# Cross attention's output projection of two batches at a time, in seven products of blocks instead of eight

## The chip, the cores and the metric

The kernel runs on one core of a Trainium2 chip. The core has five engines, each with its own in-order queue of instructions: TensorE (PE; its weight loads are listed as PEld), VectorE (DVE), ScalarE (ACT), GpSimd (POOL) and SyncE (SP), which here only issues DMA transfers. TensorE multiplies 128 x 128 blocks and writes into PSUM; the other engines read PSUM or SBUF. An instruction that needs another engine's result or a transfer waits on a semaphore at the head of its queue, and everything behind it on that queue waits too. The metric is the device time of one execution in microseconds (us), less is better. All numbers are float32.

## What is computed

Two decoder layers with the norm after each addition, for 8 batches of 128 tokens of 512 features. The part that matters here is the second layer's cross attention: 16 query heads of 96 features in 4 groups, keys and values from the context and the tokens (256 in all), an output projection, an addition and a layer norm, and after it a low-rank expert layer.

```
scores = einsum('bhqd,bksd->bhqs', q, k) / sqrt(96)
attn   = softmax(scores)
out    = einsum('bhqs,bksd->bhqd', attn, v)     # 16 heads x 96 = 1536 features
x      = layernorm(x + out @ Wo.T)              # Wo: 512 x 1536, the projection of this change
x      = layernorm(x + low_rank_experts(x))
```

## The kernel before

The program is written out in full by Python loops; the order on each engine comes from the order in the source and a scheduler that places instructions as their inputs are expected. `tc.issue_after(instruction)` ties the placing of what stands in it to an instruction. Tiles come from pools with a number of buffers per tag; a tile that reuses a buffer waits for the last reader.

The cross attention is the last stage, from about 537 us on. The loop `for b in range(B)` takes a batch in two steps `hh` of eight heads each. For each step:

- `Heads8` makes the scores on TensorE (`s_x`, line 931, 24 matmuls), `maxima` and `exps` make the softmax on DVE and ACT (lines 941 to 960), the last step of which is a transposition in blocks of 32 (line 960).
- `turn` (line 966) moves the result into the tile `pT` by 16 DMAs of 64 KB, issued by SP (in the last two batches by SP and ACT in turns). `pT` has one buffer.
- `Front` makes keys, values and queries for the next two batches in pieces (`pvx`, `pkx`, `pqx`, all through line 86), which are put between the other work by `nxt.go(n)`.

At the first step of batch b, `mix(b - 1)` finishes the batch before: `outputs` multiplies the whole `pT` by the values (`o_x`, line 976, 48 instructions) into the tile `oTx` (128 x 3 x 512, one buffer, copied out of PSUM by DVE, ACT and DVE at line 982), and `projected` multiplies `oTx` by the output weights in 12 matmuls of 512 columns (`pox`, line 993), adds the old x out of PSUM and normalizes (`add_norm`, lines 91 to 107). Each matmul is two instructions in the trace, as the data are float32. At the second step, `low_rank(b - 1)` does a piece of the low-rank layer for each of three batches: turning the tokens (`low_tokens`), scores (`low_scores`), turning the weighted heads (`low_turn`) and the last product, norm and store (`low_last`). The last two batches have an order of their own; the code after the loop finishes batches 6 and 7.

The output weights `w_X_o` are three tiles of 128 x 2048 (1 MB each), loaded by SP at line 67 when earlier weights have been used up, between 466 and 506 us, and they stay in SBUF to the end. GpSimd has no work in this stage except the small power of the norms (line 97).

Of the kernel before, what the change touches and what calls it, by code (L numbers as in the profile page):

```python
# [43 lines left out]
def decoder(ctx: ExitStack, tc: tile.TileContext, a: dict, out: bass.AP):  # L44
# [858 lines left out]
    layer.close()  # L903
    for k in ("q0", "q1", "q2"):
        wqs.append(weight4(f"X_{k}"))
    wos = [weight(f"X_o{i}").rearrange("p (c o) -> p c o", c=4) for i in range(3)]


    with stage("x1b", 2, side="right") as ap, stage("f1", 2, side="right") as fp:
# [9 lines left out]
        class Heads8:  # L919
# [42 lines left out]
            def turn(self, pT, queues=(nc.sync,)):  # L962
                e = self.e.rearrange("p (s j) h k -> p s j (h k)", s=2)
                for i in range(4):
                    for j in range(4):
                        queues[j % len(queues)].dma_start(
                            pT[32 * j : 32 * j + 32, :, i, self.h0 // 2, :], e[32 * i : 32 * i + 32, :, j, :]
                        )

# [17 lines left out]
        def projection(b, oT, between={}):  # L987

            po = bank(f"pox_{b}")
            for i in range(NX):  # L990
                n, h = divmod(i, G)
                w = wos[(h * NS + n) // 4][:, (h * NS + n) % 4, :]
                nc.tensor.matmul(po, lhsT=oT[:, n, h * P : (h + 1) * P], rhs=w, start=(i == 0), stop=(i == NX - 1))  # L993
                for piece in between.get(i, ()):
                    piece()
            return po

        def turned_low(b):
            xT = fp.tile([P, NC, P], F32, tag="xT", name=f"xTf1_{b}")
# [87 lines left out]
        def low_rank(b):  # L1087

            if b >= 2:
                low_turn(b - 2)  # L1090
            if b >= 1:
                low_scores(b - 1)
            low_tokens(b)
            if b >= 2:
                low_last(b - 2)

        def pT_tile(b):
            return ap.tile([P, 2, 4, 2, 8 * 32], F32, tag="pT", name=f"pT_x1_{b}", bufs=1)

        pTs, vs_x, oTs_x = {}, {}, {}  # L1100

        def outputs(b):
            oTs_x[b] = ap.tile([P, NS, 512], F32, tag="oT", name=f"oTx_{b}", bufs=1)
            mixed(b, vs_x.pop(b), pTs.pop(b), oTs_x[b])

        def projected(b, between={}):
            po = projection(b, oTs_x.pop(b), between)
            xs[b] = add_norm(xs[b], po, f"x1_{b}")

        def mix(b):  # L1110
            outputs(b)
            projected(b)

        for b in range(B):
            pr, j = divmod(b, 2)
            if j == 0 and b:
                front, nxt = nxt, upcoming
            toks = slice(j * P, (j + 1) * P)
            for hh in range(2):
                now = Heads8(front.qT[:, :, toks], front.kT[:, :, :, toks], 2 * hh, f"x1_{b}_{hh}")  # L1120
                now.maxima()
                now.exps(0)
                now.exps(1)
                if b < B - 2 and hh == 0:

                    nxt.go((4, 3)[j] if b < B - 3 else 2)
                    if b:
                        mix(b - 1)
                    pTs[b] = pT_tile(b)
                    now.turn(pTs[b])  # L1130
                elif b < B - 2:
                    if j == 1 and b < B - 3:

                        upcoming = Front(pr + 2)
                    now.turn(pTs[b])
                    nxt.go(2)
                    if b:
                        low_rank(b - 1)
# [187 lines left out]
def _layouts(i):  # L1326
# [47 lines left out]
    for j in range(3):  # L1374
        a[f"X_q{j}"] = _rows(wq[j])
        a[f"X_o{j}"] = _rows(wo[:, j])
    a["X_k"] = _rows(i["L1_xattn_Wk"].reshape(KV, NS, 32, D).transpose(1, 0, 2, 3).reshape(KV * XD, D))
    return {k: np.ascontiguousarray(v) for k, v in a.items()}

# [17 lines left out]
```

## Time and profile before

| what | value | how to read it |
|---|---|---|
| three runs | 876.8, 877.1, 878.6 us | median 877.12 |
| the profiled execution | 878.72 us | its span, first to last instruction, is 876.9 |
| granted TensorE clock | 0.995 | mean over the execution, 1 is full speed |
| `pqx` (line 86), 256 columns | 384 instructions, 84.9 us busy | busy time counts overlaps once |
| `pox` (line 993), 512 columns | 168 instructions, 74.1 us busy | seven batches of 24 instructions |
| `s_x` (line 931) | 768 instructions, 50.0 us busy | |
| `o_x` (line 976) | 384 instructions, 43.7 us busy | |
| `pT` on SP (line 966) | 224 issues of 64 KB | one issue keeps SP for 0.585 to 1.674 us, median 0.595 |

The profile is one execution. "Busy" of an engine is the time in which it has an instruction running; a line in the list of groups gives the program's line, engine, operation, output from inputs, shape, count, busy time, mean length of one and the idle time before them with what ended it. The chain of waits is followed back from the last instruction: at each step to what released it.

### The profile page before, as it was taken

How to read it: one execution, taken by the hardware profiler on the slowest of the kernel's cores; microseconds unless marked ns; L12 is line 12 of the kernel's file. 1: busy time of each engine (PE TensorE's matmuls, PEld its weight loads, DVE VectorE, ACT ScalarE, POOL GpSimd, SP SyncE). 2: the span in 40 equal slices, each digit the busy share in tenths (PEclk: the TensorE clock that was granted, in tenths of full speed). 3: DMA queues.
4: the chain of work that ended last, by engine and by line, in shares of the span. 5: the costliest groups of instructions: out<-in, count | busy, mean ns of one | idle time of the engine just before them, and what ended most of it. 6: DMA issues, size and time to landing. Idle time of an engine off the chain costs nothing.

```text
span 876.9 us, 17899 instructions
## 1 busy us (share of the span) xinstructions
PE 851.9 (97%) x6482; PEld 530.0 (60%) x6482; DVE 543.4 (62%) x2166; ACT 369.6 (42%) x1535; POOL 188.9 (22%) x267
## 2 busy tenths in 40 slices
PE   9999999999899999999999999999999999999996
PEld 5776655655445455555555687858475846576454
DVE  3656786776868657777778512734363545467654
ACT  3876574664223126766666403303121322224310
POOL 2500233123433214555555300000000000000000
PEclk9999999999999999999999999999999999999998
DMA  9700000130300002000004020331213121313340
GB/s 327 310 2 26 1 14 13 50 109 1 145 13 24 1 1 97 2 1 2 2 2 146 27 73 1 79 90 43 46 37 86 43 48 36 82 42 80 81 96 36
DMA packets 30073, 50.73 MB, mean 58 GB/s; under 512 B 5536, under 2 KB 22048, under 8 KB 28192
## 3 DMA queue, kind: packets, MB, share of 16 engines
q1 hardware_dynamic: 27424, 47.49, 18.1%
q10 hardware_dynamic: 2560, 2.10, 1.1%
q8 instruction: 51, 0.84, 0.4%
q14 instruction: 38, 0.31, 0.1%
HBM read 30.69 MB, written 2.10 MB: 37 GB/s over the span
## 4 chain that ended last, share of the span: by engine, by line
PE 64%; DVE 19%; ACT 11%; POOL 2%; issue 2%; DMA 1%; SPq 0%; ACTq 0%; POOLq 0%; DVEq 0%
PE pqx L86 10%; ACT e_a L197 7%; PE pox L993 7%; PE pkx L86 4%; PE pvx L86 4%; PE s_x L931 4%; PE o_x L976 4%; PE pq L86 3%; PE pk L86 3%; DVE e_a L184 3%; PE pv L86 3%; PE pof L618 2%; PE pt_a L228 2%; PE po L86 2%; PE s_a L165 2%
## 5 line engine op out<-in xcount | busy, mean ns | idle before, releaser
L197 ACT ACTIVATE e_a<-e_a,m_a 128x128 f32<-128x128 f32 (+1 forms) x512 | 184.7, 363 | 96.0 <-DVE m_a L184 96.0
L952 ACT ACTIVATE e_x<-s_x,m_x 128x256 f32<-128x256 f32 x128 | 58.7, 484 | 139.8 <-DVE m_x L942 123.4
L197 ACT ACTIVATION_READ_ACCUMULATOR e_a<-e_a,m_a 128x1 f32 x512 | 96.7, 189 | 0.0
L86 PE MATMUL pqx<-xTx,w_X_q 128*128 128x256 f32 x384 | 84.9, 380 | 0.0
L86 PEld LDWEIGHTS pqx<-xTx,w_X_q 128*128 128x128 f32 x384 | 72.6, 190 | 11.4 <-issue 1.8
L993 PE MATMUL pox<-w_X_o,oTx 128*128 128x512 f32 x168 | 74.1, 597 | 0.7 <-DVE oTx L982 0.6
L941 DVE TENSOR_REDUCE m_x<-s_x 128x4 f32<-128x1024 f32 x32 | 37.6, 1218 | 41.2 <-PE s_x L931 41.2
L97 POOL TENSOR_TENSOR rs_x<-ve_x,neghalf 128x1 f32<-128x1 f32 x7 | 3.9, 550 | 268.3 <-DVE ve_x L95 249.2
L211 POOL TENSOR_TENSOR e_a<-e_a,rc_a 128x512 f32<-128x512 f32 (+1 forms) x64 | 52.8, 847 | 33.8 <-DVE rc_a L208 18.8
L993 PEld LDWEIGHTS pox<-w_X_o,oTx 128*128 128x128 f32 x168 | 31.3, 190 | 40.9 <-issue 39.2
L228 PE MATMUL pt_a<-ident,e_a 128*128 128x128 f32 x384 | 48.4, 273 | 3.0 <-DVE m_a L184 3.0
L931 PE MATMUL s_x<-kTx,qTx 32*128 32x256 f32 x768 | 50.0, 385 | 0.8 <-ACT e_x L952 0.8
L228 PEld LDWEIGHTS pt_a<-ident,e_a 128*128 128x128 f32 x384 | 43.4, 140 | 11.9 <-issue 5.0
L184 DVE CUSTOM_DVE_ANT_0 e_a<-s_a,masks 128x128 f32<-128x128 f32 (+1 forms) x256 | 47.1, 253 | 4.4 <-PE s_a L165 3.1
L931 PEld LDWEIGHTS s_x<-kTx,qTx 32*128 32x128 f32 x768 | 39.0, 184 | 16.9 <-issue 11.7
L184 DVE CUSTOM_DVE_ANT_0 e_a<-s_a,alibi 128x128 f32<-128x128 f32 (+1 forms) x256 | 47.3, 253 | 1.4 <-PE s_a L165 1.3
L976 PE MATMUL o_x<-pT_x,vx 128*32 128x512 f32 x384 | 43.7, 595 | 1.8 <-issue 0.6
L184 DVE DVE_READ_ACCUMULATOR2_ANT m_a<- 128x1 f32 x512 | 42.6, 83 | 0.1
L960 DVE STREAM_TRANSPOSE e_x<-e_x 128x1024 f32<-128x1024 f32 x32 | 39.7, 1241 | 0.8
L165 PEld LDWEIGHTS s_a<-kbd,qT 32*64 32x64 f32 x1024 | 21.7, 131 | 29.0 <-issue 15.4
L959 DVE TENSOR_SCALAR e_x<-e_x,rc_x 128x256 f32<-128x256 f32 x128 | 36.3, 347 | 3.8 <-DVE rc_x L956 2.4
L838 ACT COPY qTx<-pqx 128x512 f32<-128x512 f32 x24 | 14.1, 595 | 55.1 <-PE pqx L86 54.8
(236 smaller groups left out, 1616.4 us busy)
## 6 DMA issues: line engine op xcount, KB each, us to landing
pT_x<-e_x SPq DMA_DIRECT2D x224, 64.0 KB, 2.0
w_X_q<-in_X_q SPq DMA_DIRECT2D x3, 1024.0 KB, 4.7
w_X_o<-in_X_o SPq DMA_DIRECT2D x3, 1024.0 KB, 4.9
w_L_Wv<-in_L_Wv SPq DMA_DIRECT2D x2, 1024.0 KB, 6.8
w_L_Wo<-in_L_Wo SPq DMA_DIRECT2D x2, 1024.0 KB, 8.6
x_in<-in_x SPq DMA_DIRECT2D x8, 256.0 KB, 9.0
ct<-in_ctx SPq DMA_DIRECT2D x8, 256.0 KB, 2.6
cT<-in_ctxT SPq DMA_DIRECT2D x4, 512.0 KB, 3.9
```

The costliest lines, as they stand in the source:

```text
L86: nc.tensor.matmul(ps, lhsT=l, rhs=r, start=(i == 0), stop=(i == n - 1))
L165: nc.tensor.matmul(s[r // 2][64 * u : 64 * u + 64, r % 2, cols], lhsT=qT[rows, 64 - 64 * part : P - 64 * part], rhs=kbd[rows, :, :keys], s ...
L184: self.scored = nc.vector.tensor_tensor_reduce(self.e[:, r, cols], s[i][:, r % 2, cols], bias(r, cols), -1.0, 3e38, ALU.add, ALU.min, self ...
L197: nc.scalar.activation(e[:, r, x, :], e[:, r, x, :], AF.Exp, scale=-1.0, bias=self.m[:, part, r, x : x + 1], accum_out=self.su[:, part, r, ...
L211: nc.gpsimd.tensor_tensor(e, e, bc(self.rc[:, part, rs, :].unsqueeze(3), list(e.shape)), ALU.mult)
L228: nc.tensor.transpose(pt[:, r, cols], self.e[:, 2 * i + r, cols], ident)
L931: nc.tensor.matmul(sc[g // 2][:, g % 2, u * 256 : (u + 1) * 256], lhsT=qT[rows, (h0 + u) * NS + n, :], rhs=kT[rows, n], start=(n == 0), st ...
L941: nc.vector.tensor_reduce(m, self.s[i], AX.X, ALU.max, negate=True)
L952: nc.scalar.activation(self.e[:, :, j, :], self.s[half][:, i, :].rearrange("p (a k) -> p a k", k=32), AF.Exp, bias=self.m[:, j : j + 1], s ...
L960: nc.vector.transpose(self.e[:, :, js, :], self.e[:, :, js, :])
L976: nc.tensor.matmul(po[32 * g : 32 * g + 32, :], lhsT=v[:, s, g * XD + 32 * n : g * XD + 32 * n + 32], rhs=pT[:, s].rearrange("p i h x -> p ...
L993: nc.tensor.matmul(po, lhsT=oT[:, n, h * P : (h + 1) * P], rhs=w, start=(i == 0), stop=(i == NX - 1))
```

## The change

Batches 0 with 1 and 2 with 3 are projected together. With the 1536 features split into two halves (the first two and the last two heads of each group), the 512 output columns into two halves, and the two batches as the rows, the product is one of 2 x 2 blocks, and it is done in seven block products with sums before and after (the Strassen-Winograd scheme) instead of eight. A block product is six matmuls of 256 columns. Batches 4 to 7 are projected as before.

The seven products need three blocks of the weights as they are (`X_ob`, laid out by the host) and four sums of blocks. The sums are formed on the chip in `form_sums`: three loads of the weights in another layout (`X_ot`) into the three slots, four subtractions on GpSimd for each slot, and three stores to a buffer in device memory. From there and from `X_ob` the products' right sides are streamed through the three slots of 8 matmuls each (`stream`). After the second pair, the plain weights `X_o` are loaded into the slots for batches 4 to 7 (`plain_outputs`).

`paired` does the seven products with the sums of the left side on GpSimd, copies of two products on ACT, and additions on DVE and GpSimd. `oTx` gets two buffers. In the loop, batch 0 ends its first step with `form_sums`, tied to the last of the first 16 DMAs into `pT`; the first step of batch 1 makes `outputs(0)` and starts the stream; the first steps of batches 2 and 4 make the outputs of the batch before and then the pair. The low-rank pieces move to the second steps of batches 2 to 5 (`LOWS`) and to batches 6 and 7.

```diff
-    wos = [weight(f"X_o{i}").rearrange("p (c o) -> p c o", c=4) for i in range(3)]
+    slots = [wp.tile([P, 2048], F32, tag="w", name=f"w_X_o_{i}") for i in range(3)]
+    wos = [t.rearrange("p (c o) -> p c o", c=4) for t in slots]
+    kept = ctx.enter_context(tc.tile_pool(name="kept", bufs=1, space=bass.MemoryType.DRAM))
+    weight_sums_kept = kept.tile([P, 4, 3, 512], F32, tag="ts", name="ts")
+    def form_sums():
+        for i, t in enumerate(slots):
+            nc.sync.dma_start(t, a["X_ot"][:, i])
+            b11, b12, b21, b22 = (t[:, j * 512 : (j + 1) * 512] for j in range(4))
+            nc.gpsimd.tensor_tensor(b11, b12, b11, ALU.subtract)
+            nc.gpsimd.tensor_tensor(b12, b22, b12, ALU.subtract)
+            nc.gpsimd.tensor_tensor(b22, b22, b11, ALU.subtract)
+            nc.gpsimd.tensor_tensor(b21, b21, b22, ALU.subtract)
+            nc.sync.dma_start(weight_sums_kept[:, :, i, :], t.rearrange("p (j o) -> p j o", j=4))
+
+    sums_flat = weight_sums_kept.rearrange("p j i o -> p (j i o)")
+    BLOCK = 6 * 256
+    T1, T3, T4, T2 = ((sums_flat, j * BLOCK) for j in range(4))
+    B11, B21, B22 = ((a["X_ob"], j * BLOCK) for j in range(3))
+    ORDER = [B11, T1, B21, T2, B22, T3, T4]
+
+    def stream(t):
+        lo, hi = 2048 * t, min(2048 * (t + 1), 7 * BLOCK)
+        while lo < hi:
+            block, off = divmod(lo, BLOCK)
+            n = min(hi - lo, BLOCK - off)
+            source, base = ORDER[block]
+            nc.sync.dma_start(slots[t % 3][:, lo - 2048 * t : lo - 2048 * t + n], source[:, base + off : base + off + n])
+            lo += n
+
+    def plain_outputs():
+        for i, t in enumerate(slots):
+            nc.sync.dma_start(t, a[f"X_o{i}"])
...
+        def paired(b0, b1):
+            o0, o1 = oTs_x.pop(b0), oTs_x.pop(b1)
+            x0, x1 = xs[b0], xs[b1]
...
+            def product(left):
+                ps = bank(f"pox_{b0}_{used[0]}")[:, :256]
+                for kk in range(6):
+                    h, n = divmod(kk, NS)
+                    t, u = divmod(used[0], 8)
+                    nc.tensor.matmul(
+                        ps, lhsT=left[:, n, h * P : (h + 1) * P], rhs=slots[t % 3][:, u * 256 : (u + 1) * 256],
+                        start=kk == 0, stop=kk == 5,
+                    )
+                    used[0] += 1
+                    if u == 7:
+                        if t < 3:
+                            stream(t + 3)
+                        elif t < 5 and not paired.last:
+                            stream(t - 3)
+                return ps
+
+            add(nc.gpsimd, s, o1[:, :, first], o1[:, :, second])
+            add(nc.gpsimd, o1[:, :, first], o0[:, :, first], o1[:, :, first], ALU.subtract)
+            nc.scalar.copy(p1, product(o0[:, :, first]))
+            nc.scalar.copy(p5, product(s))
+            add(nc.gpsimd, s, s, o0[:, :, first], ALU.subtract)
+            add(nc.gpsimd, x0[:, first], x0[:, first], p1)
+            add(nc.vector, r0[:, first], product(o0[:, :, second]), x0[:, first])
+            add(nc.gpsimd, o0[:, :, second], o0[:, :, second], s, ALU.subtract)
+            add(nc.vector, p1, product(s), p1)
+            add(nc.gpsimd, x0[:, second], x0[:, second], p5)
+            add(nc.gpsimd, x0[:, second], x0[:, second], p1)
+            add(nc.vector, r0[:, second], product(o0[:, :, second]), x0[:, second])
+            add(nc.gpsimd, x1[:, second], x1[:, second], p5)
+            add(nc.vector, p1, product(o1[:, :, first]), p1)
+            add(nc.gpsimd, x1[:, first], x1[:, first], p1)
+            add(nc.gpsimd, r1[:, second], x1[:, second], p1)
+            add(nc.vector, r1[:, first], product(o1[:, :, second]), x1[:, first])
+            if paired.last:
+                plain_outputs()
+            else:
+                stream(2)
+            for b, r in ((b0, r0), (b1, r1)):
+                mean, rs = moments(r, f"x1_{b}")
+                nc.vector.tensor_scalar(r, r, mean, rs, ALU.subtract, ALU.mult)
+                xs[b] = r
...
+        PAIRED = 4
+        LOWS = {
+            2: [lt(0), lt(1)],
+            3: [lsc(0), lsc(1)],
+            4: [lh(0), lh(1), lt(2), ll(0), lt(3), ll(1)],
+            5: [lsc(2), lsc(3), lt(4)],
+        }
...
-                    nxt.go((4, 3)[j] if b < B - 3 else 2)
-                    if b:
+                    if b > PAIRED:
+                        nxt.go((4, 3)[j] if b < B - 3 else 2)
                         mix(b - 1)
+                    elif b and not j:
+                        nxt.go(3)
+                        outputs(b - 1)
+                        nxt.go(1)
+                        paired.last = b == PAIRED
+                        paired(b - 2, b - 1)
+                    else:
+                        nxt.go((4, 3)[j])
+                        if b:
+                            outputs(b - 1)
+                        if b == 1:
+                            for t in range(3):
+                                stream(t)
                     pTs[b] = pT_tile(b)
                     now.turn(pTs[b])
+                    if not b:
+                        with tc.issue_after(now.moved.ins):
+                            form_sums()
...
-                    if b:
-                        low_rank(b - 1)
+                    for piece in LOWS.get(b, ()):
+                        piece()
...
-                    low_turn(b - 3)
-                    outputs(b - 1)
                     if b == B - 2:
+                        low_turn(B - 6)
+                        low_turn(B - 5)
+                        outputs(b - 1)
+                        low_last(B - 6)
                         low_scores(B - 4)
                         low_last(B - 5)
                     else:
+                        low_turn(B - 4)
+                        outputs(b - 1)
                         low_tokens(B - 3)
```

Here `lt`, `lsc`, `lh` and `ll` are `low_tokens`, `low_scores`, `low_turn` and `low_last`, and `add(engine, out, left, right, op)` is one `tensor_tensor` on that engine.

More of the change, by code (lines that the diff above doesn't have):

```diff
@@ L965, in turn @@
                     for j in range(4):
-                        queues[j % len(queues)].dma_start(
+                        self.moved = queues[j % len(queues)].dma_start(
                             pT[32 * j : 32 * j + 32, :, i, self.h0 // 2, :], e[32 * i : 32 * i + 32, :, j, :]
@@ L996, in projection @@
             return po
+        def paired(b0, b1):
+            o0, o1 = oTs_x.pop(b0), oTs_x.pop(b1)
+            x0, x1 = xs[b0], xs[b1]
+            first, second = slice(0, 256), slice(256, 512)
+            s = ap.tile([P, NS, 256], F32, tag="s", name=f"s_x1_{b0}", bufs=1)
+            p1, p5 = (ap.tile([P, 256], F32, tag=f"p{i}", name=f"p{i}_{b0}", bufs=1) for i in (1, 5))
+            r0, r1 = (xp.tile([P, D], F32, tag="x", name=f"x_x1_{b}") for b in (b0, b1))
+            add = lambda eng, o, l, r, op=ALU.add: eng.tensor_tensor(o, l, r, op)
+            used = [0]
+            def product(left):
[39 more added lines that the diff above has]
+                xs[b] = r
@@ L1085, in low_last @@
             last(b, low_sum(b, turned_lows.pop(b)))
[L1087 to L1095, printed above, removed]
         def pT_tile(b):
@@ L1102, in outputs @@
         def outputs(b):
-            oTs_x[b] = ap.tile([P, NS, 512], F32, tag="oT", name=f"oTx_{b}", bufs=1)
+            oTs_x[b] = ap.tile([P, NS, 512], F32, tag="oT", name=f"oTx_{b}", bufs=2)
             mixed(b, vs_x.pop(b), pTs.pop(b), oTs_x[b])
@@ L1112, in mix @@
             projected(b)
+        PAIRED = 4
+        lt, lsc, lh, ll = ((lambda b, f=f: lambda: f(b)) for f in (low_tokens, low_scores, low_turn, low_last))
+        LOWS = {
[4 more added lines that the diff above has]
+        }
         for b in range(B):
@@ L1376, in _layouts @@
         a[f"X_o{j}"] = _rows(wo[:, j])
+    o = np.concatenate([a[f"X_o{j}"].reshape(P, 4, 2, 256) for j in range(3)], axis=1).reshape(P, 2, 6, 2, 256)
+    o = o.transpose(0, 1, 3, 2, 4)
+    a["X_ob"] = np.concatenate([o[:, 0, 0], o[:, 1, 0], o[:, 1, 1]], axis=1).reshape(P, -1)
+    a["X_ot"] = o.reshape(P, 4, 3, 512).transpose(0, 2, 1, 3).reshape(P, 3, 2048)
     a["X_k"] = _rows(i["L1_xattn_Wk"].reshape(KV, NS, 32, D).transpose(1, 0, 2, 3).reshape(KV * XD, D))
```

## The prediction

> **What bounds the kernel now.** I read the page's busy table first, then the chain of waits from 560 us on, then the timelines of SP and DVE, then the groups by shape on POOL, because the change adds work on SP and POOL while it takes work off PE.
>
> ```profile
> PE 851.9 (97%) x6482; PEld 530.0 (60%) x6482; DVE 543.4 (62%) x2166; ACT 369.6 (42%) x1535; POOL 188.9 (22%) x267
> ```
> ```profile
> 567.41 6.91 PE pqx L86 x32
> 574.32 5.31 PE o_x L976 x48
> 579.63 10.50 PE pox L993 x24
> 590.12 2.80 PE s_x L931 x48
> ```
> The first line is busy time by engine; the others are the chain that ended last (start, length, what). PE is never idle for more than a fraction of a microsecond here, so a product taken out shortens the kernel by its own length, and a wait put in front of PE lengthens it by its own length. The projection of one batch (pox) is 10.5 us.
>
> ```profile
> 550.15 22.55 SPq L966 DMA_DIRECT2D pT_x<-e_x  x32
> 572.80 0.53 SPq L795 DMA_DIRECT2D cT<-in_ctxT  x1
> ```
> ```profile
> 560.17 1.25 DVE L960 STREAM_TRANSPOSE e_x<-e_x 128x1024 f32<-128x1024 f32 x1
> ```
> ```profile
> pT_x<-e_x SPq DMA_DIRECT2D x224, 64.0 KB, 2.0
> w_X_o<-in_X_o SPq DMA_DIRECT2D x3, 1024.0 KB, 4.9
> ```
> These are SP's timeline, DVE's timeline and the DMA issues with their time from issue to landing. SP hands out the 32 pieces of pT for batch 0 at 22.55/32 = 0.705 us each: 16 for the first half of the heads, 16 for the second. The second half's input is ready at 561.4 (DVE's transpose), just when the first 16 are through (550.15 + 11.3). The last issue starts at about 572.1 and lands 2.0 later, at 574.1; o_x, which reads all of pT, starts at 574.3. So SP is as close to the path here as PE is: it has a margin of some 0.2 us.
>
> **The change, part by part.** *The product.* The chain's four projections of batches 0 to 3 take 10.50, 10.57, 10.50 and 10.58, in all 42.15 us. The two pairs take 2 x 42 matmuls of 256 columns. Such a matmul (two instructions) takes 6.91/16 = 0.432 us in the chain's pqx line, with a new stationary block each time, as here. 84 x 0.432 = 36.3 us. Saved on PE: 5.9 us.
>
> *form_sums on the SP queue.* This decides. In the changed program SP's order for batch 0 is: 16 pieces of pT, three loads of X_ot, three stores of the sums, and only then the other 16 pieces of pT. Each store waits for four chained POOL instructions on its slot, and what stands behind a waiting SP instruction waits with it. That SP itself waits on other engines is in its waits:
>
> ```profile
> SPq L966 <- DVE e_x L960: 68.2, 8, 35.2
> ```
> (68.2 us in eight waits.) POOL's price is in these rows (count, busy us, mean ns, idle before):
>
> ```profile
> L473 POOL TENSOR_TENSOR vw<-vw 128x512 f32<-128x512 f32 x8 | 10.2, 1269 | 18.7 <-DVE vw L472 18.5
> L670 POOL TENSOR_TENSOR k<-k,lnv 128x512 f32<-128x512 f32 x8 | 10.2, 1274 | 0.6
> L443 POOL TENSOR_TENSOR ex<-co,top 128x512 f32<-128x512 f32 x8 | 8.4, 1050 | 27.2 <-DVE top L435 27.1
> ```
> The first two have two full operands, as the new subtractions have; the third has one broadcast. I take 1.27, with 1.05 as the lower end. Nothing in front of SP's loads changes, so they issue at 561.4. Slot 0 lands 4.9 later, at 566.3; 1 MB at the 354 to 409 GB/s that the trace shows for 5 to 30 us is under 3 us, so slots 1 and 2 are there before POOL asks. POOL: 12 x 1.27 + 11 x 0.08 for the step from one to the next (0.6/8 in the second row) = 16.1, and it ends at 582.4. The last store's issue costs about 0.5 (the cT line). The 16 pieces then issue from 582.9 to 594.2, the last one at 593.5, landing 2.0 later: 595.5.
>
> What is queued behind it on PE: o_x of batch 0. In the changed program the second scores of batch 1 are begun first (13 of 24 matmuls, 13/24 x 2.80 = 1.5 us), then PE stands in front of o_x from 574.3 + 1.5 = 575.8. Stall: 595.5 - 575.8 = 19.7 us, with nothing on PE's in-order queue to fill it. Bounds: with 1.05 for the subtraction and the loads 0.5 faster, 19.7 - 2.6 - 0.5 = 16.6; with stores that land late and hold back the pT pieces that reuse their semaphores, by as long as one more 1 MB transfer (4.9), 24.6. DVE and ACT run dry too, but behind PE.
>
> *The clock after the stall.* No stretch of this trace has a long idle in mid-kernel. The nearest rows are at its start:
>
> ```profile
> 1.45 3.69 PE L297 MATMUL nobody<-idle 128*128 128x512 f32 x4 [1.45 <-DVE idle L294]
> 626.90 10.57 PE L993 MATMUL pox<-w_X_o,oTx 128*128 128x512 f32 x24
> ```
> Four instructions of 512 columns take 3.69 after idleness, and 4 x 10.57/24 = 1.76 later on: 1.9 us lost. The granted clock over 0 to 5 us reads 1.00, by which nothing would be lost. I take 1.9, with 0 and 3.8 (twice the start's) as ends. The Trainium skill ("TensorE: Matmul & The Clock Gate", "What's actually happening") says that the array falls to half rate after an idle window of about 3.4 us and is released after one busy one; by it alone an estimate is 3.4/2 = 1.7 us lost, by the clock row zero, and the sum would be 0.2 or 1.9 lower.
>
> A second rule speaks against the change: the same skill ("DMA: Bandwidth & Descriptors", the part on where the 2 us goes) has semaphore waits sit on the issuing sequencer, not in the DMA engines. The wait row above agrees as far as it goes; were it otherwise, the stall would be the few issues in front alone, which is the first rival below.
>
> *Inside a pair.* Set the end of the second batch's o_x to 0. One pvx follows (2.78), then seven products of 6 x 0.432 = 2.59: they start at 2.8, 5.4, 8.0, 10.6, 13.1, 15.7, 18.3 and end at 20.9. POOL's 768-column operations I scale to 1.27 x 1.5 = 1.9 and its 256-column ones to 0.65. The sum s is ready at 0.7 + 1.9 = 2.6, wanted at 5.4. s minus o0 can start when product 2 ends (8.0) and is ready at 9.9, wanted at 10.6. o0 minus s starts at 11.2, behind two small additions, and is ready at 13.1, wanted at 13.1: margin zero, so up to 0.5 may show. Streamed slot 3 may issue when matmul 8 is done (6.3), two issues of some 0.35, and lands by 11.9 (4.9 after the second), wanted at matmul 25 (13.2). Slot 4 follows 3.5 later and is wanted 3.5 later. The cover is 1.3 us; without it, that much per slot shows. DVE ends both norms at about 23.7, 2.8 after the last product; before, 3.1 after (637.5 to 640.6). I take 0 for a pair, with 0 to 2 as ends. ACT's two copies (0.37 each by the 256-column copies of xTf) and DVE's five small additions lie between products. The X_o loads behind the second pair have a whole batch until their use; those that go away ahead were issued by 506 us, off the path.
>
> *The moved low-rank pieces.* Their PE work is the same. low_last(2) and low_turn(2) now fall into batch 6, where ACT hands out 16 pieces of pT and PE already waits:
>
> ```profile
> 821.07 2.86 PE L931 MATMUL s_x<-kTx,qTx 32*128 32x256 f32 x44 [0.77 <-ACT e_x L952]
> ```
> DVE gets one more add and norm there (0.69 + 0.69 + 0.18 + 0.15 + 0.73 waiting + 0.55 = 3.0), part of it ahead of the maximum for which ACT waits in the middle of its issues; but PE has about 1 us more of its own there too. I take 0.5, with 0 and 3.0 as ends.
>
> **Sum.** -5.9 + 19.7 + 1.9 + 0 + 0.5 = +16.2 us. The profiled execution's span is 876.9 and its time 878.7, so the span becomes 893.1 and the time 894.9. The three runs' median, 877.1, lies 1.6 below the profiled time, so I forecast 893.3, say 893.
>
> **Rivals.** (1) *SP does not hold the second half of pT back*: then only three loads and three stores are issued ahead of it, 6 x 0.5 = 3.0, o_x starts at 577.3 and the stall is 1.5, too short for the clock. 877.1 - 5.9 + 1.5 + 0.5 = 873.2, faster. For it: the saving is on the path. Against: SP's order and its waits. It wins if POOL's twelve were done before 562, and their input lands at 566. Chance 0.07. (2) *The streams are late as well*: both pairs wait for slots 3 to 5, at most one landing (4.9) for each pair, since 1 MB has to arrive within 16 matmuls (6.9 us) on a queue that pT shares. 893.3 + 9.8 = 903. For it: the 1.3 us cover. Against: DMA is busy for 0.2 to 0.5 of this stretch only. Chance 0.10. (3) *The stall is partly hidden*: POOL at 1.05 and loads 0.5 faster give 16.6, no clock loss, nothing in the tail: 877.1 - 5.9 + 16.6 = 887.8. Chance 0.17; my own forecast has 0.66.
>
> **How the numbers follow.** The likeliest case's ends are 877.1 - 5.9 + 16.6 = 887.8 and 877.1 - 5.9 + 24.6 + 3.8 + 2 + 3 = 904.6, which needs all ends at once; I cut it to 900, where stall and clock are at their ends one at a time. Below I go to 885 to take in rival 3 with a quicker queue. Below 885 lies rival 1, above 900 most of rival 2. A measurement of this kernel can tell 0.2% (1.8 us) from no change: faster is rival 1 with 0.07, same needs a stall of 5.5 by chance, 0.02, slower 0.91.
>
> **What would show it.** Right: PE idle for some 19 us ahead of batch 0's o_x, released by the DMA into pT; SP waiting for POOL three times; twelve subtractions of 1.27; from there to the pairs the same steps as before, and 36.3 us in pox for batches 0 to 3. Wrong: o_x of batch 0 starting before 580, subtractions far under 1.05, or idle of several us between the seven products.

## The result, and the profile after

The changed kernel takes 891.5 us (median of five runs, 890.5 to 895.1), the kernel before 878.1 in the same comparison (five runs, 876.8 to 879.1): ratio 1.0164, 95% interval 1.0140 to 1.0189. It is slower, by 1.6%. The profiled execution of the changed kernel is its slowest run, 895.09 us with a span of 893.3, so that the spans (876.9 and 893.3) lie 16.4 apart and the medians 13.4; times inside a profile are compared with spans below. Three of the experiments' profiles fell into executions that the chip held up from end to end (their spans are 1234 to 2221 us), so those kernels are read from their other runs' times, and two of them from a second profile.

The busy table of the changed kernel (busy us, share of the span, instructions):

```profile
PE 848.2 (95%) x6554; PEld 544.3 (61%) x6554; DVE 553.0 (62%) x2172; ACT 371.1 (42%) x1539; POOL 226.7 (25%) x299
```

PE is busy for 3.7 us less than before, 95% of a longer span where it was 97%. POOL does 37.8 us more, DVE 9.6 more. Where PE stood still is one line of its timeline (start, length, line, operation, output from inputs, shapes, count, and in brackets the idle time ahead and what ended it):

```profile
568.04 7.07 PE L86 MATMUL pqx<-xTx,w_X_q 128*128 128x256 f32 x32
575.04 1.99 PE L964 MATMUL s_x<-kTx,qTx 32*128 32x256 f32 x26
597.88 8.29 PE L1009 MATMUL o_x<-pT_x,vx 128*32 128x512 f32 x48 [20.85 <-DMA pT_x<-e_x]
606.09 1.57 PE L964 MATMUL s_x<-kTx,qTx 32*128 32x256 f32 x22
```

Before, `pqx` was followed by `o_x` of batch 0 without a gap, and `o_x` took 5.36 us:

```profile
567.25 7.07 PE L86 MATMUL pqx<-xTx,w_X_q 128*128 128x256 f32 x32
574.27 5.36 PE L976 MATMUL o_x<-pT_x,vx 128*32 128x512 f32 x48
```

Now 26 of the 48 score instructions stand in between, PE is idle for 20.85 us, and `o_x` takes 8.29. SP's timeline of the same stretch, and its waits from 545 to 600 us (total, times, longest), say what the transfer into `pT` was behind:

```profile
550.90 10.79 SPq L999 DMA_DIRECT2D pT_x<-e_x  x16
561.74 1.56 SPq L912 DMA_DIRECT2D w_X_o<-in_X_ot  x3
573.68 11.13 SPq L918 DMA_DIRECT2D ts<-w_X_o  x3
584.90 11.31 SPq L999 DMA_DIRECT2D pT_x<-e_x  x16
596.25 0.58 SPq L933 DMA_DIRECT2D w_X_o<-in_X_ob  x1
```
```profile
SPq L918 <- POOL w_X_o L917: 14.7, 3, 5.4
SPq L918 <- DMA w_X_o<-in_X_ot: 4.9, 1, 4.9
```

From 561.7 to 584.9 SP issues six DMAs. It first waits 4.9 us for a load to land; then each store (line 918) waits for the last of its slot's four subtractions (line 917), three waits of 14.7 us in all. The input of the second sixteen pieces was there all that time: DVE had transposed it by 562.2 (561.4 before). POOL's timeline, first and last of the twelve:

```profile
568.26 1.27 POOL L914 TENSOR_TENSOR w_X_o<-w_X_o 128x512 f32<-128x512 f32 x1 [59.16 <-DMA w_X_o<-in_X_ot]
569.61 1.35 POOL L915 TENSOR_TENSOR w_X_o<-w_X_o 128x512 f32<-128x512 f32 x1
...
581.66 1.26 POOL L916 TENSOR_TENSOR w_X_o<-w_X_o 128x512 f32<-128x512 f32 x1
583.00 1.26 POOL L917 TENSOR_TENSOR w_X_o<-w_X_o 128x512 f32<-128x512 f32 x1
```

And the stretches of 20 us around it (PE, PEld, DVE, ACT, POOL busy with counts; then PE's granted clock, the DMA share and GB/s):

```profile
580.00:600.00 20.00, 2.12 (x12) 0.69 (x16) 1.63 (x2) 0.00 (x0) 4.03 (x4) 0.50 0.65 196
600.00:620.00 20.00, 20.00 (x119) 13.52 (x112) 8.96 (x18) 5.99 (x20) 0.00 (x0) 0.90 0.65 203
```

After the stall PE comes back at half its clock: in steps of 1 us the granted clock reads 0.50 from 597 to 603, 0.59 in the next and 1.00 from 604 on. The pairs themselves run as they should: the first one's products follow one another from 639.50 to 657.89 without a wait, and between the stall and the scores of batch 6 PE's largest waits are two of 0.73 us, for DVE's copy ahead of the last third of an `o_x`; the order of the change has them with eight products too.

### The profile page after: what moved, and what is told of

Read it like the earlier page. It is cut to its first block, busy times and chain, and to the rows that moved or that the text cites. A ratio compares the mean times of both kernels' runs of the same rounds, so it can differ in the third digit from the quotient of the medians.

```text
span 893.3 us, 18158 instructions
## 1 busy us (share of the span) xinstructions
PE 848.2 (95%) x6554; PEld 544.3 (61%) x6554; DVE 553.0 (62%) x2172; ACT 371.1 (42%) x1539; POOL 226.7 (25%) x299
## 4 chain that ended last, share of the span: by engine, by line
PE 55%; DVE 21%; ACT 11%; SPq 4%; POOL 4%; DMA 3%; issue 2%; ACTq 0%; POOLq 0%; DVEq 0%
PE pqx L86 7%; ACT e_a L197 6%; PE pox L1047 4%; SPq L999 4%; PE pq L86 3%; DVE e_a L184 3%; PE o_x L1009 3%; PE pkx L86 3%; PE pk L86 3%; PE pv L86 3%; PE s_x L964 3%; PE pof L618 2%; PE pt_a L228 2%; PE po L86 2%; PE pox L1026 2%; DMA pT_x<-e_x 2%
## 5 line engine op out<-in xcount | busy, mean ns | idle before, releaser
L1009 PE MATMUL o_x<-pT_x,vx 128*32 128x512 f32 x384 | 46.2, 628 | 23.0 <-DMA pT_x<-e_x 20.9
L964 PE MATMUL s_x<-kTx,qTx 32*128 32x256 f32 x768 | 47.3, 383 | 0.0
L992 DVE TENSOR_SCALAR e_x<-e_x,rc_x 128x256 f32<-128x256 f32 x128 | 43.8, 405 | 3.8 <-DMA pT_x<-e_x 2.2
L1009 PEld LDWEIGHTS o_x<-pT_x,vx 128*32 128x32 f32 x384 | 12.8, 114 | 51.9 <-issue 47.2
L165 PE MATMUL s_a<-kbd,qT 32*64 32x256 f32 (+1 forms) x1024 | 34.9, 335 | 2.1 <-ACT pT_a L229 1.0
L1039 POOL TENSOR_TENSOR s_x<-oTx 128x768 f32<-128x768 f32 x2 | 3.6, 1809 | 119.8 <-DVE oTx L1015 119.8
```

The lines of the kernel that those rows point to most:

```text
L165: nc.tensor.matmul(s[r // 2][64 * u : 64 * u + 64, r % 2, cols], lhsT=qT[rows, 64 - 64 * part : P - 64 * part], rhs=kbd[rows, :, :keys], s ...
L964: nc.tensor.matmul(sc[g // 2][:, g % 2, u * 256 : (u + 1) * 256], lhsT=qT[rows, (h0 + u) * NS + n, :], rhs=kT[rows, n], start=(n == 0), st ...
L992: nc.vector.tensor_scalar(e, e, self.rc[:, j : j + 1], None, ALU.mult)
L1009: nc.tensor.matmul(po[32 * g : 32 * g + 32, :], lhsT=v[:, s, g * XD + 32 * n : g * XD + 32 * n + 32], rhs=pT[:, s].rearrange("p i h x -> p ...
```

## The experiments

### The sums where SP and GpSimd have nothing to do

```diff
+        nxt, upcoming = Front(1), None
+        with tc.issue_after(nxt.loaded.ins):
+            form_sums()
...
-                    if not b:
-                        with tc.issue_after(now.moved.ins):
-                            form_sums()
```

(`loaded` is the load of the second pair's context.)

> The three loads, twelve subtractions and three stores of the weight sums stand right behind the load of the second pair's context, at about 515 us, where GpSimd has nothing to do and SP's queue nothing to issue until 550; all else is as in the change. Theory (the stall is the second half of batch 0's weights of attention held behind the stores in SP's queue): the sums are stored by 540, o_x of batch 0 waits for no transfer, and the 20.85 us of stall and the 2.93 us that the cold clock took from the o_x behind it are both gone: about 23.8 us under the change, 867 to 871 us. Rival A (the streams and sums cost by their traffic to and from device memory, wherever they lie): no better than before, 877 or more. Rival B (a wait elsewhere takes the stall's place, because the pairs come earlier and their blocks don't): 872 to 882, with a wait for w_X_o in the products.

Measured: 870.2 us, ratio to before 0.9903 (0.9888 to 0.9918), span 868.7. It beats both kernels. SP's timeline:

```profile
515.33 1.37 SPq L912 DMA_DIRECT2D w_X_o<-in_X_ot  x3
526.71 11.02 SPq L918 DMA_DIRECT2D ts<-w_X_o  x3
537.82 0.58 SPq L933 DMA_DIRECT2D w_X_o<-in_X_ob  x1
...
550.47 22.63 SPq L999 DMA_DIRECT2D pT_x<-e_x  x32
```

The same three stores wait for the same subtractions, and nothing that anybody needs stands behind them; the 32 pieces of `pT` go through in one go, in 22.63 us as before (22.55). `o_x` of batch 0 starts at 574.71 and takes 5.36. Both the stall and the cold clock are gone, Rival A falls, and no product waits for its weights, so Rival B does as well.

### The sums left out

This kernel forms no sums, and its products read blocks that are not summed.

```diff
-    sums_flat = weight_sums_kept.rearrange("p j i o -> p (j i o)")
+    sums_flat = a["X_ot"].rearrange("p i x -> p (i x)")
...
-                            form_sums()
```

> The sums of the weights are left out: no loads for them, no subtractions, no stores, and the streams read the unsummed blocks instead, the same bytes in the same pieces. The products, the streams, the additions on the left-hand sides and the order of the low-rank pieces stay. Theory: with the stores the whole loss is gone, and what stays is the seven products' gain: 867 to 871 us, and the same as the run with the sums made early within 2 us. Rival A (pairs, streams or the moved low-rank pieces cost by themselves): 875 or more. Rival B (the sums also cost when early, through contention): the run with early sums is more than 2 us slower than this one.

Measured: 871.0 us, 0.9904 (0.9887 to 0.9922): the same as with the sums made early. Formed in the quiet stretch, the sums cost nothing that can be measured; formed where the change has them, they cost the whole of the difference.

### The sums behind the second half of the moves

> The sums stay in the cross attention but behind the second half of batch 0's moves in SP's queue, not between the halves. Theory: o_x of batch 0 no longer waits, and what is behind the stores is late instead, which is now the six first stream pieces, batch 1's 32 moves and the load of the third pair's context: stores end at about 597, the moves of batch 1 land at about 625, where PE reaches o_x of batch 1 at about 608; so a stall of 15 to 19 us in pvx or o_x of batch 1, with 1 to 3 us of cold clock behind it: 884 to 890 us. Rival (only batch 0's second half is short of time, later moves have slack): no stall over 3 us, 867 to 872.

The edit puts the same call behind the second step's `turn` of batch 0. Measured: 892.7 us, 1.0153 (1.0137 to 1.0169), span 891.8. `o_x` of batch 0 no longer waits, as the theory has it, and the stall moved to the next thing behind the stores. Timelines of PE and of SP:

```profile
621.73 8.29 PE L86 MATMUL pvx<-w_X_v,cT 128*128 128x384 f32 x16 [20.75 <-DMA cT<-in_ctxT]
```
```profile
583.54 11.11 SPq L918 DMA_DIRECT2D ts<-w_X_o  x3
...
601.37 15.05 SPq L999 DMA_DIRECT2D pT_x<-e_x  x16
616.46 0.58 SPq L795 DMA_DIRECT2D cT<-in_ctxT  x1
```

The load of the third pair's context is issued at 616.46 (at 573.20 with early sums) and PE waits 20.75 us for it; `pvx` takes 8.29 where it takes 5.33 at full clock. I had expected 15 to 19, and 884 to 890 us: the sixteen moves ahead took 15.05 us instead of some 10, because SP waited 4.1 us in between for stream pieces to land. The rival, that later moves have slack, falls.

### The stores on GpSimd's own queue

```diff
-            nc.sync.dma_start(weight_sums_kept[:, :, i, :], t.rearrange("p (j o) -> p j o", j=4))
+            nc.gpsimd.dma_start(weight_sums_kept[:, :, i, :], t.rearrange("p (j o) -> p j o", j=4))
```

> The three stores are issued from GpSimd's own queue, at the place of the change; loads and all else stay on SP. Theory: SP passes from the three loads straight to the second half of batch 0's moves, and o_x of batch 0 waits less than 2 us; what still holds SP is the first stream piece of each buffer, which must wait until that buffer is stored, up to about 588, and so batch 1's moves come some 15 us later than without it and o_x of batch 1 waits 3 to 9 us: 871 to 880 us. Rival A (GpSimd's subtractions beside VectorE are what makes batch 0 late, whichever queue stores): o_x of batch 0 still waits over 10 us, 880 to 892. Rival B (nothing else is held): 867 to 870.

Measured: 886.1 us, 1.0077 (1.0058 to 1.0097), outside what the theory allowed. The same kernel a second time:

> The kernel with the stores on GpSimd's queue again, 886.1 us where the theory said 871 to 880, for a profile at the usual clock (the first one was taken at a granted clock of 0.557 throughout and shows none of the waits). Theory, corrected: SP passes the loads, o_x of batch 0 waits under 3 us, and the stall sits at batch 1, in pvx for the third pair's context or in o_x, 10 to 18 us of it, because the stream pieces that stand next on SP wait for the buffers' stores. Rival A (subtractions beside VectorE make batch 0 late): o_x of batch 0 itself waits over 5 us, and the second half's moves are issued late because e_x is late. Either way 884 to 888 us.

Measured: 887.3 us, 1.0101 (1.0081 to 1.0120). PE's timeline, and SP's waits from 562 to 581 us:

```profile
581.92 6.97 PE L1009 MATMUL o_x<-pT_x,vx 128*32 128x512 f32 x48 [7.17 <-DMA pT_x<-e_x]
...
620.91 7.96 PE L1009 MATMUL o_x<-pT_x,vx 128*32 128x512 f32 x48 [6.20 <-DMA pT_x<-e_x]
```
```profile
SPq L999 <- DMA w_X_o<-in_X_ot: 7.1, 3, 3.8
```

Two stalls in place of one. The second is the one I had in mind: the stream pieces on SP wait for the stores to land (9.6 us in one wait) and hold batch 1's moves back. The first is neither theory nor rival: the second half's scaled weights were there at 561.8, and SP had only the three loads ahead of them, but three of the sixteen issues waited for these loads *to land*, 7.1 us in all. Sixteen issues took 17.36 us instead of 11.3. So moving the stores was not enough: here three of the sixteen moves behind the loads had to wait for the loads as well. What ties them together is in the last section.

### Fewer subtractions

Nine of twelve subtractions are left out, one for each slot stays; the sums are not the ones that the products need.

> Nine of the twelve subtractions are left out, one for each buffer stays; loads, stores, streams and their places are those of the change. Theory (the stall is the chain load, subtractions, stores, 16 moves): the chain is shorter by 9 x 1.34 = 12.1 us, and so is the stall of o_x of batch 0: 8 to 10 us of it, and 1 to 3 us of cold clock: 877 to 881 us. Rival (the stores or the loads themselves take the time, the subtractions lie beside them): stall of 15 us or more, 885 to 892.

Measured: 890.4 us, 1.0133 (1.0117 to 1.0149). Taken by itself this would refute the theory. But in the program that came out, SP's order differs: two loads, two stores, and only then the third load, so that its landing was added to the chain. The second try writes out the order of the change:

```diff
-            nc.sync.dma_start(weight_sums_kept[:, :, i, :], ...)
+            with tc.issue_after(load.ins):
+                form_sums.done = nc.sync.dma_start(weight_sums_kept[:, :, i, :], ...)
...
-                    now.turn(pTs[b])
+                    with nullcontext() if b else tc.issue_after(form_sums.done.ins):
+                        now.turn(pTs[b])
```

> Three of the twelve subtractions again (one for each buffer, nine left out), and now with SP's order of the change written out: three loads, three stores, sixteen moves. In the run before it the third load stood behind the first two stores, so its landing was added to the chain, and that run (890.4 us) didn't price the subtractions. Theory (chain of load, subtractions, stores, moves): the last store is ready when the third load has landed and one subtraction is done, at about 570 to 573, some 12 us sooner than in the change; o_x of batch 0 waits 8 to 11 us and loses 1 to 3 us to the cold clock: 877 to 882 us. Rival (loads and stores, not the subtractions, take the time): o_x of batch 0 waits over 14 us, 885 to 891.

Measured: 885.1 us, 1.0078 (1.0064 to 1.0092), span 884.2. PE's timeline:

```profile
588.94 7.61 PE L1008 MATMUL o_x<-pT_x,vx 128*32 128x512 f32 x48 [12.01 <-DMA pT_x<-e_x]
```

The time lies at the lower end of the rival's range, the stall between theory and rival: it falls by 8.8 us, not by 12.1. The three loads land one after another, and the subtractions start at 567.10, 570.53 and 573.99; with one subtraction for each slot it is the third load, not POOL, that sets the last store. So of the 20.85 us, 8.8 are the nine subtractions, and 12.0 are the loads, one subtraction and the moves behind them; a faster subtraction could take at most its own 1.27 from that.

### Eight products at the pairs' places

The four projections as before the change, from weights that stay in the slots, without sums, streams or additions, but in the new order: two projections where a pair stands, two buffers of `oTx`, the low-rank pieces where the change has them.

```diff
-                        paired(b - 2, b - 1)
+                        projected(b - 2)
+                        projected(b - 1)
```

> The projections of batches 0 to 3 again as eight products (two of 24 matmuls with 512 columns for a pair) from weights that stay in the buffers, but at the pairs' places and with the changed order of the low-rank pieces; no sums, no streams, no additions. It prices the order alone. The run with early sums is 8.2 us shorter than before by the profiled spans, of which the products explain 5.9. Theory: the rest, 2 to 3 us, is the order of the low-rank pieces, which the prediction had put at +0.5: 875.5 to 877.5 us where before is 878.9. Rival A (the order costs nothing or a little): 878.5 to 880. Rival B (the pairs gain more than their matmuls, by the order of weights or fewer closings): as Rival A, with the pairs' stage shorter in the run with early sums by over 7 us.

Measured: 875.0 us, 0.9964 (0.9951 to 0.9976), span 872.5. The order alone is worth 4.0 us. From the first scores of batch 0 to those of batch 6 it takes 241.70 us where the kernel before takes 245.78, and from there to the end 94.59 and 94.29. In the kernel before, PE's timeline has scores between the thirds of an `o_x`:

```profile
620.73 0.70 PE L931 MATMUL s_x<-kTx,qTx 32*128 32x256 f32 x4
...
623.47 0.70 PE L931 MATMUL s_x<-kTx,qTx 32*128 32x256 f32 x4
...
626.15 0.70 PE L931 MATMUL s_x<-kTx,qTx 32*128 32x256 f32 x4
```

Such a group of four takes 0.70 us; in the new order all 48 stand together and take 2.87, which is 0.24 for four. In return PE now waits ahead of the last third of the same `o_x`:

```profile
609.41 1.92 PE L1010 MATMUL o_x<-pT_x,vx 128*32 128x512 f32 x16 [0.74 <-DVE oTx L1016]
```

From start to start, `o_x` and the 48 scores of this place took 10.38 us before (20.88, less 10.50 for the projection between them) and take 9.04 now (6.23 and 2.81): 1.34 less with the wait counted, and as much at the second such place (at 711 before), 2.7 in all. The other 1.4 is a sum of small things that no run prices singly. Two projections back to back take 20.69 where the single ones took 10.49 and 10.50, which is 0.6 for both pairs; a wait of 0.65 us ahead of batch 4's `o_x` is gone; one low-rank output (0.27 and 1.02 us) moved behind the scores of batch 6, into a stretch where PE had waited (0.77 and 0.60 us in the profile before); against that stand new waits of 0.25 and 0.38 us. The pairs, in this kernel and with early sums:

```profile
613.95 20.76 PE L1027 MATMUL pox<-w_X_o,oTx 128*128 128x512 f32 x48
634.64 2.87 PE L965 MATMUL s_x<-kTx,qTx 32*128 32x256 f32 x48
```
```profile
614.70 2.75 PE L1047 MATMUL pox<-w_X_o,oTx 128*128 128x256 f32 x12
...
625.12 8.04 PE L1047 MATMUL pox<-w_X_o,oTx 128*128 128x256 f32 x36
633.09 2.87 PE L964 MATMUL s_x<-kTx,qTx 32*128 32x256 f32 x48
```

From the first product to the scores behind it: 634.64 - 613.95 = 20.69 for two projections, 633.09 - 614.70 = 18.39 for a pair. Seven products instead of eight save 2.30 us for a pair, 4.6 in all; the medians of the two kernels lie 4.8 apart. Rival B, that the pairs gain more, falls.

### GpSimd beside VectorE, with no transfer

To the kernel with early sums it adds twelve subtractions on a buffer that nothing reads.

```diff
                 now.maxima()
+                if not b and hh:
+                    ...
+                    nc.gpsimd.tensor_tensor(scratch[:, :8], now.m, now.m, ALU.subtract)
+                    for _ in range(12):
+                        nc.gpsimd.tensor_tensor(scratch[:, :512], scratch[:, 256:], scratch[:, :512], ALU.subtract)
                 now.exps(0)
```

> The early sums, and besides twelve more subtractions of GpSimd, 128x512 each and chained, on a buffer that nothing reads, from the moment the second half of batch 0 has its maxima (about 567 us): the place of the change's subtractions, with no transfer and nothing more on SP. It prices GpSimd beside VectorE alone. Theory (part of the loss of the change's place is VectorE's scaling, four 128x256 in 4.3 to 5.4 us beside GpSimd's subtractions against 1.14 without them): each of the two groups of four takes 2 to 5.5 us, the second half's moves are issued 3 to 7 us later, and o_x of batch 0 waits 3 to 7 us for them, then loses 1 to 2 us to the clock: 873 to 879 us. Rival (the slow scaling goes with the transfers of the loads, not with GpSimd): the groups take 1.1 to 1.3 us and the time is that of the early sums, 869 to 871.

Measured: 880.1 us, 1.0012 (1.0003 to 1.0021), span 878.2: 9.5 us more than without them, a little above the theory's range and far from the rival's. They started at 554, not at 567 (I had taken batch 1's maxima for batch 0's), and so met batch 0's own scaling. Timelines of DVE, POOL and PE:

```profile
555.97 5.01 DVE L992 TENSOR_SCALAR e_x<-e_x,rc_x 128x256 f32<-128x256 f32 x4
...
562.82 4.90 DVE L992 TENSOR_SCALAR e_x<-e_x,rc_x 128x256 f32<-128x256 f32 x4
...
574.36 1.14 DVE L992 TENSOR_SCALAR e_x<-e_x,rc_x 128x256 f32<-128x256 f32 x4 [0.23 <-DMA pT_x<-e_x]
```
```profile
554.19 16.07 POOL L1215 TENSOR_TENSOR scratch<-scratch 128x512 f32<-128x512 f32 x12
```
```profile
580.76 7.61 PE L1009 MATMUL o_x<-pT_x,vx 128*32 128x512 f32 x48 [6.48 <-DMA pT_x<-e_x]
```

Four scalings of DVE take 4.9 to 5.0 us while GpSimd subtracts and 1.14 when it is done. With both groups late, the second half is transposed at 569.0, where it was 561.9 with early sums, and `o_x` waits 6.48 us and then loses 2.25 to the clock. The slow scaling needs no load of weights beside it: the rival falls. In the change itself the twelve subtractions slowed DVE in the same way (two groups of 4.33 and 5.38), but those were batch 1's scalings, done by 580.4, and PE stood still until 597.88 for another reason.

### A third pair

On top of the early sums, batches 4 and 5 are paired too, at the place of the projection of batch 5, with their low-rank pieces moved behind it.

```diff
-                        projected(b - 2)
+                        paired.last = True
+                        paired(b - 3, b - 2)
                     first = now
```

> The early sums with a third pair, batches 4 and 5, at the place of the projection of batch 5; the low-rank pieces of batch 4 move behind it, and the plain weights for batches 6 and 7 are loaded after the third pair. Theory: a pair is 2.3 us shorter than two projections back to back (20.69 against 18.39 us), the end of the kernel has other work for PE in the meantime, and the plain weights land within 8 us, beside scores and outputs of batch 6 and 7: 866.5 to 869.5 us, against 870.2 with two pairs. Rival A: the plain weights' loads wait on SP for the pair's last product and hold batch 7's moves behind them, and o_x of batch 7 or the projection of batch 6 waits: 871 to 880. Rival B: batch 4's low-rank pieces lengthen the end: 870 to 873.

Measured: 879.4 us, 1.0013 (1.0004 to 1.0023): 9 us worse than two pairs. PE's timeline:

```profile
809.82 10.18 PE L1047 MATMUL pox<-w_X_o,oTx 128*128 128x256 f32 x36 [7.89 <-POOL oTx L1039]
```

None of the three expectations named this wait. Here ACT hands out sixteen of `pT`'s pieces itself, until 798.8 (not until 802, as the next expectation has it); then its eight exponentials come first, which start at 801.7, when DVE has the maxima, and its copies of the first two products (done at 796) come at 805.3; POOL's additions with these copies wait, and behind them in POOL's order stands the left-hand side of the fifth product. The next kernel has the copies on VectorE (`nc.vector.tensor_copy` in place of `nc.scalar.copy` for the last pair):

> The third pair again, with the two copies of its first products on VectorE instead of ScalarE. In the run before it ScalarE issued sixteen of batch 6's moves from its own queue from 785 to 802, so the copies came at 805, GpSimd's additions behind them were late, and the fifth product waited 7.89 us for a left-hand side that stood behind these additions in GpSimd's queue; the matmuls after it lost another 2.1 us to the clock. Theory: with the copies on VectorE that wait falls under 2 us and the cold clock with it: 867 to 871 us. Rival A (VectorE, which scales and normalises in that stretch beside GpSimd, is as late as ScalarE was): a wait of 3 us or more stays in the products, 872 to 879. Rival B (the third pair loses at the end of the kernel, not in the pair): no wait in the products, and still 872 or more.

Measured: 876.6 us, 0.9973 (0.9962 to 0.9985). The same kernel a second time:

> The third pair with its copies on VectorE once more, 876.6 us where 867 to 871 was expected, for a profile at the usual clock (the first was taken at a granted clock of 0.656 throughout). Left as theory: VectorE's and GpSimd's work beside each other keeps the products waiting, 3 to 6 us in the third pair and 1 to 3 us of cold clock. Rival: the products run without a wait, and the end of the kernel, from the projection of batch 6 on, is longer by 5 us or more than in the run with two pairs. Either way 875 to 878 us.

Measured: 876.4 us, 0.9976 (0.9962 to 0.9989). The waits are still in the pair, now split, by PE's timeline:

```profile
803.50 4.54 PE L1047 MATMUL pox<-w_X_o,s_x 128*128 128x256 f32 x12 [4.25 <-POOL s_x L1039]
809.47 8.04 PE L1047 MATMUL pox<-w_X_o,oTx 128*128 128x256 f32 x36 [1.43 <-POOL oTx L1039]
```

5.7 us of waiting and 1.8 of cold clock (4.54 for a product that takes 2.75) for a gain of 2.3. The rival has a part as well: from the projection of batch 6 on, the end takes 48.0 us where two pairs take 46.2, with a new wait of 1.85 us for a norm on DVE. In this place DVE and POOL have other work in front of the pair's additions, a norm of the low-rank output among it; an order that puts the additions first was not tried.

## Why the prediction was right, and where it was not

The forecast was 893.0 us and slower; measured 891.5. The mechanism is the one it named. Its terms, one by one:

- *SP holds the second half of `pT` back.* Right, and shown from three sides: without the sums (871.0) and with the sums early (870.2) the stall is gone, and with the sums one step later (892.7) it moves to what then stands behind the stores. Stall 19.7 forecast, 20.85 measured. The subtractions took 16.0 (16.1 forecast). Slot 0 landed 6.5 us after its issue, not 4.9, and the three loads took 8.2 in the median. That `pT`'s pieces beside them are the reason is not shown: with early sums, where no piece is under way and one load of 0.5 MB stands just ahead, it was 6.0 and 8.0. That the slots behind the first would be there before POOL asks held with four subtractions for each; with one for each it did not. The upper bound's case, moves that wait for an earlier transfer with the same semaphore, did not come in the change, but it did with the stores on GpSimd's queue.
- *Clock after the stall: 1.9.* Mis-sized, 2.93. In the other runs the matmuls behind an idle stretch lost 2.96 after 20.75 us, 2.25 after 12.0 and after 6.5, 2.60 after 6.2, 2.14 after 7.9, 1.61 after 7.2 and 1.79 after 4.3, so that it hardly follows the length of the wait. The granted clock shows it here (0.50), which it did not at the start of the kernel. The Trainium skill ("TensorE: Matmul & The Clock Gate", "What's actually happening") has half rate end after one busy window of about 3.4 us, by which an estimate was 1.7; the 2.93 lost in `o_x` are what 5.9 us at half rate lose, and the measurement decides.
- *The product: -5.9.* Mis-sized, -4.6 against eight products in the same place. The 84 x 0.432 leave out 0.25 for each pair's ends (18.39 against 18.14), and two projections back to back take 20.69, not twice 10.5.
- *Inside a pair: 0.* Right for two pairs: no product waits, for weights or for POOL. The margin of zero that the forecast saw for the fifth product is real: in the changed kernel POOL ends its left-hand side at 649.87 and the product starts at 649.93, and in the third pair, where ACT and POOL came late, PE waited there.
- *The moved low-rank pieces: +0.5.* This is the step that failed: "Their PE work is the same." The order was worth -4.1 by the profiles. The work is the same, but the forecast had no term for the order that comes out around the pieces: whether the scores are cut into groups of four at 0.70 us each (2.7 of the 4.1, and no matter of the low-rank pieces at all), whether projections stand back to back, and whether an output lies on the path or in a gap.
- *The sum.* By the spans the terms are +20.85 + 2.93 - 4.6 - 4.1 = +15.1, and 0.8 us lie ahead of the place of the change (the first scores start at 537.69 instead of 536.90); 0.5 of the 16.4 remain, about what it costs that the stall cuts the 48 scores ahead of it into 26 and 22 (1.99 + 1.57 where they take 2.87 together). These are spans of the slowest of five runs; by the medians the change cost 13.4, and no profile shows where a median run is shorter. That the forecast of +16.2 was met is luck in the sizes: a stall and a clock loss that were 2.2 too small and a product's gain that was 1.3 too large stood against an order that was priced 4.6 too dear.

Of the rivals, SP passing on (873.2) did not happen, but its time is nearly that of the versions in which nothing stands in its way (870.2 and 871.0). Late streams (903) fall: no product waits for `w_X_o` in any profile of a kernel that streams its weights. The partly hidden stall (887.8) falls too: the stall was 20.85 us, not 16.6, and the clock took its part.

## What to carry to other kernels

Before a helper's DMAs go on a queue, write down what stands behind them: a store that waits for a chain on another engine makes every later issue on that queue wait for that chain, and the price appears at whoever needs one of them first. Preparation of weights belongs where both its queue and its engine are idle; the same six transfers and twelve subtractions cost 21 us of stall at 561 us and nothing at 515. And when a change also moves other work, run the move alone: here it was nearly as large (4.1 us) as the gain that the change was made of (4.6).

## What was not expected of the hardware

- Beside GpSimd's 128x512 subtractions, VectorE's 128x256 scaling from SBUF to SBUF took up to 1.43 us instead of 0.35, about as long as one GpSimd instruction, and up to 1.97 in the third pair beside its 128x768 ones of 1.81; its transposes (1.25) and its copies out of PSUM did not change, and GpSimd's steps stayed at 1.34. The Trainium skill ("SBUF — State Buffer", "SBUF: two separate sides") says that a VectorE operation in a two-port mode and a GpSimd operation lock each other out for whole instructions. The runs agree for VectorE, where sixteen microseconds of GpSimd cost the kernel 9.5; that GpSimd is held up in turn they do not show.
- Sixteen 64 KB moves behind three 1 MB loads on SP's queue waited 7.1 us in three waits until those loads had landed, though they read and write other tiles. The trace names what ties them together, and it is the program's, not the queue's: SP's transfers report their landing on eight semaphores in turn, a transfer waits until the one before it on its semaphore has landed, and the three moves that waited (the sixth to the eighth) stand on the semaphores of the three loads. Moves on semaphores of their own were not tried.
- Four score matmuls between other matmuls take 0.70 us from the first's start to the last's end, four of a row of 48 take 0.24.
